# Last expert layer: groups of seven batches and one in place of six and two, denser scatters, one row tile less per group

## The chip, the cores and the metric

The kernel runs on one core of a Trainium2 chip. The metric is the device time of one execution in microseconds (us). The core has five engines that matter here: TensorE (PE, matmuls; PEld are its weight loads), VectorE (DVE), ScalarE (ACT), GpSimd (POOL) and SyncE (SP, which only issues DMAs). Each works through its own instructions in order. DMAs are issued from the queues of SP, ACT and POOL; the indirect ones (scatter and gather by row numbers) are issued from POOL.

## What is computed

The reference is a model of two layers over x of 8 batches x 512 tokens x 256 features. Layer 0 is sparse attention and a feed-forward layer of 32 experts with given choices. Layer 1 is a full attention, then another attention with 32 heads, then a mixture of 16 experts, which picks four per token by its own logits. Cut to the part that the change concerns:

```python
x = x + o @ wo                                   # the last attention, all 8 batches
h = _rms(x, ff_ln_w)
logits = h @ wg                                  # 16 experts
topv, topi = jax.lax.top_k(logits, TOP_K)        # four per token
gate = jax.nn.softmax(topv, -1)
a = silu(h @ w1[e]) * (h @ w3[e]);  y = a @ w2[e]   # for each chosen expert e
return x + sum over the four of gate * y
```

Every token goes to four experts, so 8 x 512 x 4 = 16384 rows of 256 numbers are computed, grouped by expert.

## The kernel before

Tokens are handled in tiles of 128, four to a batch (NT = 4). The kernel runs through its stages one after the other: layer 0's attention, `middle` (layer 1's first attention, with layer 0's experts between its steps), `attention2` (the last attention), and `experts1` (its experts).

**How rows get to experts.** `places` (L302) turns the choices of a group of tokens into row numbers, so that each expert's rows lie together and each expert starts on a new tile of 128 rows. It compares choices with expert numbers (L310), sums over tokens with a scan (L318), subtracts a triangle product (L328), does some twenty small operations on 16 columns, adds and masks on POOL (L355, L356) and reduces (L359). Its width is experts x tiles x choices: 16 x 24 x 4 = 1536 columns for six batches, 16 x 8 x 4 = 512 for two. `scatter` (L367) then writes 128 tokens for one of the four choices to their rows in DRAM, `row_tiles` (L380) runs the experts over tiles of 128 rows, and `gather` (L375) fetches the results back, 128 tokens and one choice at a time. One batch needs 4 x 4 = 16 scatters and 16 gathers.

**Pacing.** Each scatter and gather waits for the instruction that `ex["pace"]` held when it was written (L363): in `attention2` the latest exponential (L1225), in `row_tiles` the latest Silu (L404) or the latest copy of turned rows (L413).

**Groups.** The layer's experts run over two groups of batches (L44): batches 0 to 5, then 6 and 7. `R1` (L45) is the number of row tiles of each, and is fixed: tokens x choices / 128, plus 16 for the experts' started tiles, so 6 x 16 + 16 = 112 and 2 x 16 + 16 = 48. `R0` (L46) is the same for layer 0 with 32 experts: 96. All tiles are computed, filled or not.

**attention2.** For each batch there are eight steps (`sg`) of four heads. Their main work is written in a fixed order: scores (L1211), softmax (L1221 on VectorE, L1225 on ACT, L1232 on VectorE), transposes (L1262), values (L1282), output (L1290, L1291). Between its parts `serve` (L1315) lets other work go on. There are two lists. `side` holds what the next steps need: `queries`, `keys`, `kv_values`, `output`, and from step 4 on the `prologue` of the next batch. `slow` holds `after(b)` of finished batches: `gating` (L1383: norm, logits, the four choices, gates) and, after the last batch of group 0, `by_expert` (L1425), that is `places` in one go and then the scatters, one per step of the generator. Each call of `serve` makes one step of `side`, or of `slow` if `side` is empty, and every second call one more step of `slow`.

`rotated` (L1146) makes rotated queries and keys: two products on TensorE (L1154), four on VectorE (L1155, L1156), a difference and a sum on POOL (L1159, L1160), and eight small DMAs on SP (L1164). On POOL the scatters stand in the same queue as these.

**experts1** (L1445). First come `gating` of batch 7, the load of all expert weights (16 DMAs on SP, L1460), and `by_expert` of group 1. Then `row_tiles` runs over the tiles of group 0 and of group 1 in one sequence. A tile is loaded (L389), turned (L392, L394), multiplied with the weights of its expert (L402), passed through Silu and a product (L404, L405), turned (L411, L413), multiplied (L419) and stored (L421, L422); three tiles are in flight. The generator stops twice per tile. From the end of group 0's tiles on (L1504), each stop makes one step of `combine(0)` (L1469): one gather, and 15 gathers later its addition (L1476). At the first row of each batch, ACT issues the loads of `xr` and `acc` (L1487, L1488; two buffers each), and after a batch's last addition come two operations (L1479, L1480) and the output's store on SP (L1481). What is left of `combine(0)` after the last tile, and then all of `combine(1)`, follows behind the tiles. At the moment of the switch `combine(0)` is started twice, so there is one gather more than needed.

Of the kernel before, what the change touches and what calls it, by code (L numbers as in the profile page):

```python
# [21 lines left out]
B, S, D = 8, 512, 256  # L22
NT = S // P
# [11 lines left out]
E0, K0 = 32, 4  # L35
B0 = 4
# [4 lines left out]
SC2 = 1.0 / 8.0  # L41
E1, K1 = 16, 4

GROUPS = [range(0, B - 2), range(B - 2, B)]  # L44
R1 = [len(g) * NT * K1 + E1 for g in GROUPS]  # L45
R0 = B0 * NT * K0 + E0  # L46


def shape_constants():
# [110 lines left out]
def program(ctx: ExitStack, tc: tile.TileContext, a: dict, out: bass.AP):  # L160
# [53 lines left out]

    rows1 = [[dp.tile([n * P, D], F32, name=f"rows1_{w}{g}", tag=f"rows1_{w}{g}") for w in "xy"] for g, n in enumerate(R1)]
    rows0 = [dp.tile([R0 * P, D], F32, name=f"rows0_{w}", tag=f"rows0_{w}") for w in "xy"]

# [910 lines left out]
    def attention2():  # L1128

        with ExitStack() as cx:  # L1130
# [171 lines left out]
            def after(b):  # L1302

                yield from gating(b, wk, lambda: w2.tile([P, 2, S], F32, name="hf", tag="ts", bufs=1), (pT, "T"), (pmm, "mm"))
                for gi, g in enumerate(GROUPS):
                    if b == g[-1]:
                        yield from by_expert(gi, wk, pair, (pmm, "mm"))

            side, slow, count = [], [], [0]

            def step(todo):
                if todo and next(todo[0], StopIteration) is StopIteration:
                    todo.pop(0)

            def serve(n=1):  # L1315

                for _ in range(n):
                    count[0] += 1
                    step(side or slow)
                    if count[0] % 2:  # L1320
                        step(slow)

            last, oTs = None, []
# [18 lines left out]
                return PT  # L1342

            for b in range(B):
                for sg in range(8):
                    if sg < 7:
                        side.insert(0, queries(b, sg + 1))
                    if sg == 1:
                        side.append(kv_values(b, 1))
                    if sg == 2:  # L1350
                        side.insert(0, keys(b, 1))
                    if sg == 4 and b + 1 < B:
                        side.append(prologue(b + 1))
                    PT1 = second_half() if last else None
                    serve()
                    a0 = scores_a(b, sg, 0)
                    if last:
                        pair_values(0, last[2])
                    lb = scores_b(b, sg)
                    serve()  # L1360
                    PT0 = exponentials()
                    turn(PT0, *a0, lb, 0)
                    serve()
                    a1 = scores_a(b, sg, 1)
                    if last:
                        pair_values(1, PT1)
                        if last[1] % 2:
                            side.append(output(last[0], last[1], oTs))
                            oTs = []
                    serve(2)  # L1370
                    while sg < 7 and ("q", sg + 1) not in state[b] or sg == 7 and side:
                        step(side)
                    last = (b, sg, PT0, a1, lb)
# [9 lines left out]
    def gating(b, pool, hT, psT, psm):  # L1383
# [24 lines left out]
        for i in range(NT):  # L1408
            nc.vector.max(m8[:, i, :], lg[:, i, :])
            nc.vector.max_index(i8[:, i, :], m8[:, i, :], lg[:, i, :])  # L1410
        for gi, g in enumerate(GROUPS):
            if b in g:
# [12 lines left out]
    def by_expert(gi, pool, big, psm):  # L1425

        g, pu, ne = GROUPS[gi], ex["pu"][gi], E1
        nt = len(g) * NT
# [16 lines left out]
    def experts1():  # L1445


        with ExitStack() as cx:
# [12 lines left out]
            for _ in last:  # L1461
                pass
            ng = len(GROUPS[-1]) * NT * K1 * E1
            for _ in by_expert(len(GROUPS) - 1, cp, lambda n: cp.tile([P, ng], F32, name=n, tag=n), (po, "o")):
                pass
# [83 lines left out]
```

## Time and profile before

| | us |
|---|---|
| median of 3 runs (lowest, highest) | 5092.31 (5092.24, 5099.65) |
| the profiled execution | 5130.46 |
| its span, first to last instruction | 5128.8 |
| busy: PE, PEld, DVE, ACT, POOL | 4519.2, 2521.0, 2935.3, 2138.2, 1219.0 |
| mean granted clock of TensorE | 0.934 |
| end of batch 5, 6, 7 of `attention2` (last L1291) | 4034.4, 4291.7, 4499.0 |
| last matmul | 5070.7 |
| start of the first and of the last gather of `experts1` | 4910.8, 5118.8 |

The profile is of one execution. A line such as `L402 PE MATMUL g<-wall,xT` names the line of the kernel, the engine, the operation, and output and inputs by the program's names. A bracket such as `[2.89 <-DVE lf L1232]` says that the engine was idle for 2.89 us before it, and what ended that. The ends of matmuls are modelled, not seen. A granted clock of 1.00 is the full clock of TensorE, 0.5 the half. A line that begins with two times and a colon is a stretch of the span, with its length and each engine's busy time in it.

### The profile page before, as it was taken

What the parts mean: (1) busy time and instruction counts of PE and PEld (TensorE: products, weight loads), DVE (VectorE), ACT (ScalarE), POOL (GpSimd) and SP (SyncE); (2) the same over time, 40 slices, a digit from 0 to 9 for tenths busy, and PEclk for the clock granted to TensorE, in tenths of its full rate; (3) what the DMA queues carried; (4) which work ended last, traced back from release to release, by engine and by line L of the source; (5) the groups of instructions that cost most, each with busy time, mean ns of one, the idle gap of its engine ahead of it and who ended that gap; (6) DMA issues with size and microseconds to landing.
All of it is one profiled execution on the core that took longest, in us unless ns stands there. A gap on an engine that the chain in (4) does not pass through costs nothing.

```text
span 5128.8 us, 74283 instructions
## 1 busy us (share of the span) xinstructions
PE 4519.2 (88%) x25326; PEld 2521.0 (49%) x25326; DVE 2935.3 (57%) x8302; ACT 2138.2 (42%) x5688; POOL 1219.0 (24%) x1441
## 2 busy tenths in 40 slices
PE   5898999899999987897869999999999999959994
PEld 3444444444444443564435555555555555536652
DVE  3656565656566563434547666676767766622235
ACT  0243434343433433552216555555555545513331
POOL 3223232423131211004222111111201133220046
PEclk7898999999999988998989999999999999979997
DMA  2200000000011203333111011111101112152255
GB/s 60 92 16 26 8 27 7 28 8 27 8 56 42 88 3 116 110 99 87 35 70 32 25 32 26 28 26 27 36 22 29 29 49 63 47 206 88 87 159 174
DMA packets 199732, 281.76 MB, mean 55 GB/s; under 512 B 64912, under 2 KB 151312, under 8 KB 198464
## 3 DMA queue, kind: packets, MB, share of 16 engines
q1 hardware_dynamic: 175984, 208.70, 13.5%
q0 software_dynamic: 18480, 50.49, 3.1%
q10 hardware_dynamic: 4896, 17.83, 0.9%
q8 instruction: 207, 3.39, 0.3%
q14 instruction: 165, 1.35, 0.1%
HBM read 155.69 MB, written 109.15 MB: 52 GB/s over the span
## 4 chain that ended last, share of the span: by engine, by line
PE 61%; DVE 19%; ACT 6%; issue 5%; POOL 4%; DMA 3%; SPq 0%; another core or an unknown queue 0%; ACTq 0%; DVEq 0%; POOLq 0%
PE g L402 6%; PE pt L1262 5%; PE py L1290 5%; PE ps L1211 4%; DVE lf L1232 4%; PE ps L701 4%; PE pf L837 3%; PE po L1282 3%; PE o L419 3%; PE pq L1154 3%; ACT lf L1225 3%; PE po L810 2%; DVE lf L1221 2%; PE pf L842 2%; PE pt L636 1%
## 5 line engine op out<-in xcount | busy, mean ns | idle before, releaser
L858 ACT ACTIVATE e<-pf 128x512 f32<-128x512 f32 x896 | 464.3, 602 | 692.6 <-PE pf L848 287.6
L1225 ACT ACTIVATE lf<-lf,nm 128x512 f32<-128x512 f32 (+3 forms) x1024 | 566.7, 554 | 352.0 <-DVE nm L1221 342.6
L1221 DVE CUSTOM_DVE_ANT_0 lf<-ps,caus 128x512 f32<-128x512 f32 (+3 forms) x1024 | 449.7, 485 | 136.0 <-PE ps L1211 131.2
L709 DVE TENSOR_REDUCE bm<-ps 128x32 f32<-128x512 f32 (+1 forms) x704 | 403.3, 633 | 199.6 <-PE ps L707 198.9
L1262 PE MATMUL pt<-ident,lf 128*128 128x128 f32 x2560 | 379.7, 283 | 98.3 <-ACT PT L1268 48.2
L1211 PE MATMUL ps<-kT,qT 64*128 64x512 f32 (+3 forms) x2048 | 454.1, 466 | 0.1
L1232 DVE TENSOR_SCALAR lf<-lf,nm 128x512 f32<-128x512 f32 (+3 forms) x1024 | 434.1, 481 | 7.3
L1262 PEld LDWEIGHTS pt<-ident,lf 128*128 128x128 f32 x2560 | 290.7, 143 | 292.0 <-ACT PT L1268 133.6
L402 PE MATMUL g<-wall,xT 128*128 x1024 | 413.1, 526 | 11.7 <-DVE sg L405 5.6
L837 PE MATMUL pf<-XT,KT 32*128 32x512 f32 x1280 | 296.1, 685 | 75.2 <-DVE tm L780 66.9
L1160 POOL TENSOR_TENSOR tc<-tc,ts 128x512 f32<-128x512 f32 x80 | 103.4, 1292 | 1052.2 <-issue 633.5
L1282 PE MATMUL po<-PT,VT 128*64 128x384 f32 (+3 forms) x2048 | 330.5, 441 | 0.1
L701 PE MATMUL ps<-KT,qT 32*128 32x256 f32 (+3 forms) x2048 | 265.8, 504 | 60.9 <-ACT e L858 47.9
L376 POOL DMA_INDIRECT yk<-rows_y,pu x193 | 194.4, 1007 | 501.3 <-ACT y L421 343.3
L1211 PEld LDWEIGHTS ps<-kT,qT 64*128 64x128 f32 x2048 | 219.5, 187 | 155.3 <-issue 111.3
L405 DVE TENSOR_TENSOR sg<-sg,g 128x256 f32<-128x256 f32 (+1 forms) x256 | 94.9, 371 | 338.4 <-ACT sg L404 301.3
L1154 PE MATMUL pq<-hT,wq 128*128 128x512 f32 x512 | 260.0, 621 | 6.8 <-DVE ts L1156 5.9
L404 ACT ACTIVATE sg<-g 128x256 f32<-128x256 f32 (+1 forms) x256 | 88.2, 345 | 385.7 <-PE g L402 283.2
L1290 PE MATMUL py<-wo,oT 128*128 128x256 f32 x1024 | 240.3, 387 | 0.8 <-DVE x L1291 0.8
L1268 ACT COPY PT<-pt 128x512 f32<-128x512 f32 x256 | 148.6, 580 | 214.6 <-PE pt L1262 202.0
L1282 PEld LDWEIGHTS po<-PT,VT 128*64 128x64 f32 x2048 | 144.9, 136 | 187.7 <-issue 156.0
L402 PEld LDWEIGHTS g<-wall,xT 128*128 128x128 f32 x1024 | 177.7, 193 | 110.5 <-issue 80.2
(317 smaller groups left out, 7953.4 us busy)
## 6 DMA issues: line engine op xcount, KB each, us to landing
xt<-rows_x SPq DMA_DIRECT2D x256, 128.0 KB
rows_y<-y SPq DMA_DIRECT2D x256, 128.0 KB
qT<-tc SPq DMA_DIRECT2D x512, 64.0 KB
wall<-in_we SPq DMA_DIRECT2D x32, 768.0 KB
kT<-tc SPq DMA_DIRECT2D x128, 64.0 KB
xr<-spill ACTq DMA_DIRECT2D x9, 512.0 KB
acc<-spill ACTq DMA_DIRECT2D x9, 512.0 KB
xb<-in_x SPq DMA_DIRECT2D x8, 512.0 KB
```

The source lines that it names most:

```text
L402: nc.tensor.matmul(g, xT[:, k, :], wall[:, bass.ds(e, 1), k * 2 * I:(k + 1) * 2 * I], start=k == 0, stop=k == 1)
L701: nc.tensor.matmul(ps[hq][:, g * n:(g + 1) * n], qT[rows(hq), hh, g0 + g, :], kt[rows(hq), 0, hh, 64:64 + n], start=g == 0, stop=False, sk ...
L837: nc.tensor.matmul(ps[hq], kt[rows(hq), 0, hh, 64 + j * P:64 + (j + 1) * P], x[rows(hq), hh].rearrange("p g t -> p (g t)"), start=True, st ...
L858: ex["pace"] = nc.scalar.activation(e, ps[hq], AF.Exp, scale=SC0)
L1154: nc.tensor.matmul(pq, w[:, k, col + c * P:col + (c + 1) * P], hT[:, k, :], start=k == 0, stop=k == 1)
L1211: nc.tensor.matmul(ps[h][:, o:o + n], qT[rows, pr, i * P:(i + 1) * P], kT[rows, pr, :n], start=True, stop=True)
L1221: nc.vector.tensor_tensor_reduce(out=lf, in0=ps[h][:, o:o + n], in1=caus[:, S - n:], scale=-SC2, scalar=BIG, op0=ALU.add, op1=ALU.min, acc ...
L1225: ex["pace"] = nc.scalar.activation(lf, lf, AF.Exp, scale=-1.0, bias=nm[:, 0, u:u + 1], accum_out=nm[:, 1, u:u + 1])
L1232: nc.vector.tensor_scalar(lf, lf, nm[:, 1, u:u + 1], None, ALU.mult)
L1262: nc.tensor.transpose(pt[:, j * P:(j + 1) * P], x, ident)
L1282: nc.tensor.matmul(po[64 * h:64 * h + DH2, j * P:], v[:, j, 2 * pr + h, :], PT[h][:, j, j * P:], start=j == 0, stop=j == NT - 1, skip_grou ...
L1290: nc.tensor.matmul(py[:, u, :], oTs[c][:, (i + u) * P:(i + u + 1) * P], wo2[:, 2 * (sg - 1) + c, :], start=c == 0, stop=c == 3)
```

## The change

Group 0 has the batches 0 to 6, group 1 only batch 7. `places` for group 0 is then 16 x 28 x 4 = 1792 columns wide, for group 1 256. Both `R1` and `R0` lose one tile per group: 7 x 16 + 15 = 127 and 16 + 15 = 31, in sum 158 for 160, and 95 for 96. (16 experts share out a multiple of 128 rows, so at most 15 tiles more are started than filled.) `by_expert` of group 0 starts after batch 6, not 5; its scatters are 112 instead of 96, and all lie in batch 7. In batch 7 `serve` makes one more step of `slow` at each call: one at every call, and another at every second. Group 1 has 16 scatters and 16 gathers, for 32 and 32.

```diff
-GROUPS = [range(0, B - 2), range(B - 2, B)]
-R1 = [len(g) * NT * K1 + E1 for g in GROUPS]
-R0 = B0 * NT * K0 + E0
+GROUPS = [range(0, B - 1), range(B - 1, B)]
+R1 = [len(g) * NT * K1 + E1 - 1 for g in GROUPS]
+R0 = B0 * NT * K0 + E0 - 1
...
-            side, slow, count = [], [], [0]
+            side, slow, count, late = [], [], [0], [False]
...
                 for _ in range(n):
                     count[0] += 1
                     step(side or slow)
-                    if count[0] % 2:
+                    if late[0] or count[0] % 2:
+                        step(slow)
+                    if late[0] and count[0] % 2:
                         step(slow)
...
             for b in range(B):
+                late[0] = b == B - 1
                 for sg in range(8):
```

In the changed program's GpSimd order the instructions of batch 6 are those of an ordinary batch; in batch 7 the rotations follow runs of 14, 4, 7, 19, 17 and 19 scatters, and 28 scatters come after the last.

## The prediction

> **What bounds the kernel now.** I read the page first, then the windows by batch of the last attention, then the timeline inside one batch, then the end of the expert stage. The page's chain is mostly TensorE:
>
> ```profile
> PE 61%; DVE 19%; ACT 6%; issue 5%; POOL 4%; DMA 3%; SPq 0%; another core or an unknown queue 0%; ACTq 0%; DVEq 0%; POOLq 0%
> ...
> L376 POOL DMA_INDIRECT yk<-rows_y,pu x193 | 194.4, 1007 | 501.3 <-ACT y L421 343.3
> ```
>
> The change touches three stretches. First, batches 6 and 7 of the last attention. These windows end where x has its last product added (L1291): batch 5, an ordinary one, then 6, then 7. The columns are the length, the busy time and count of PE, weight loads, DVE, ACT and POOL, the granted clock, DMA share and GB/s.
>
> ```profile
> 3811.90:4034.40 222.50, 211.35 (x1106) 126.69 (x1105) 153.87 (x521) 128.64 (x407) 33.48 (x26) 1.00 0.11 27
> 4034.40:4291.70 257.30, 233.19 (x1114) 135.88 (x1113) 171.99 (x540) 131.32 (x407) 88.59 (x87) 0.94 0.17 51
> 4291.70:4499.00 207.30, 190.15 (x996) 113.53 (x994) 130.75 (x434) 115.70 (x362) 58.74 (x57) 0.97 0.16 47
> ```
>
> Batch 6 is 34.8 us longer than batch 5 with the same matmuls, and its clock is lower. It holds the ordering of group 0 (`places`) and 55 scatters; batch 7 has 41 scatters and no prologue of a next batch. Why a scatter costs anything is seen inside batch 6:
>
> ```profile
> 4145.78 0.96 POOL L369 DMA_INDIRECT rows_x<-x,pu  x1 [2.31 <-ACT lf L1225]
> ...
> 4146.58 3.61 DVE L1232 TENSOR_SCALAR lf<-lf,nm 128x384 f32<-128x384 f32 x4
> ...
> 4146.77 1.27 POOL L1160 TENSOR_TENSOR tc<-tc,ts 128x512 f32<-128x512 f32 x1
> 4147.99 1.26 POOL L1159 TENSOR_TENSOR tc<-tc,ts 128x512 f32<-128x512 f32 x1
> ...
> 4150.15 1.09 PE L1262 MATMUL pt<-ident,lf 128*128 128x128 f32 x4 [2.89 <-DVE lf L1232]
> ```
>
> The scatter waits for its pacing exponential, the rotation (L1160, L1159) stands behind it on GpSimd, and so it lands on the four normalisations, which take 3.61 us here and 1.14 us elsewhere; TensorE waits 2.89 us and then has the half clock for 6.8 us. In the attention's timeline a 128x384 normalisation takes 416 ns (median of 128) where GpSimd does nothing, 416 ns (27) beside a scatter, and 1418 ns (99) beside a tensor_tensor. So the scatters themselves take nothing from VectorE; the rotations they displace do.
>
> Second and third, the expert stage: steady row tiles, group 1's tiles with the gathers of group 0 among them, and the tail (same columns).
>
> ```profile
> 4578.00:4911.00 333.00, 333.00 (x1323) 205.35 (x1323) 93.52 (x221) 112.66 (x331) 0.20 (x1) 1.00 0.28 88
> 4911.00:5071.00 160.00, 143.68 (x543) 86.50 (x541) 76.73 (x176) 46.57 (x138) 91.28 (x94) 0.97 0.64 187
> 5071.00:5129.00 58.00, 0.00 (x0) 0.00 (x0) 32.40 (x56) 0.15 (x1) 38.04 (x36) 0.53 0.52 161
> ```
>
> TensorE is full in the first; a tile takes 3.02 us (start to start of L402). In the tail only gathers are left, and they set the end.
>
> **Part by part.** The sum is made against the profiled execution (span 5128.8, 5130.46 us with what lies around it), which is 38.2 us over the median of 5092.31; I carry the difference over unchanged.
>
> *One tile less, three times.* Layer 0's tiles at the end of their run follow each other in 1.82 us on a TensorE without gaps (2331.9 to 2333.7): -1.8. Layer 1 loses two, at 3.02: **-6.0**. Each takes one load and one store on SP with it (0.32 and 0.38 us of issue), which hide behind the tiles. The zero fills stay 12 and 20.
>
> *Batch 6* loses ordering and scatters. Its GpSimd order becomes batch 5's, so its length should: 222.5 for 257.3, **-34.8**.
>
> *Batch 7* takes the ordering of seven batches and 112 scatters. The ordering's DVE time, from batch 6's rows: L310 2.91, three scans 3.75, three L328 2.07, L359 2.73, together 11.5; some 17 small ones 2.9; and four L1232 that take 3.37 for 1.14 beside L355/L356, 2.2. That is 16.6, and with the wide ones times 7/6, 18.5. VectorE is the releaser of TensorE's waits there, so it lies on the path: **+18.5**. The scatters: of batch 6's 34.8, 18.2 are left for eight rotations displaced. Batch 7 already has displaced rotations; its clock of 0.97 (6 us) and about 6 us more of waits than batch 5 make some 10 us. After the change it has the same seven rotations after the ordering's start, behind runs of 4 to 19 scatters instead of 1 to 10. Bounds: all rotations slip clear of the normalisations, -10; cost in proportion to the scatters (10 x 112/41), +17. I take 0: the nearest row is batch 7 itself, the number of rotations is unchanged, and a scatter beside a normalisation costs it nothing. GpSimd then has 112 x 1.27 = 142 us of scatters, about 27 of rotations and others and 8 of the ordering, 177 of some 226: a rotation can stand up to ten scatters (13 us) late, while its qT is needed about 20 us on, after 5.6 us of DMA issue. That cover is thin; if it goes, it is the third rival.
>
> [...]
>
> *Front of the expert stage.* 32 scatters become 16 and end 16 x 1.27 = 20.3 us earlier. Until 4543 the expert weights load at about 400 GB/s, and that is unchanged. Behind it TensorE stands:
>
> ```profile
> 4557.25 1.88 PE L402 MATMUL g<-wall,xT 128*128 x4
> 4569.13 0.69 PE L411 MATMUL pt<-ident,sg 128*128 128x128 f32 x2 [10.00 <-issue]
> ```
>
> Six tiles take from 4545.9 to 4577.9 where 3.02 us each would give 4560.9: 17 us lost. ACT's L404 comes 15 us after its matmul was recorded, with no cause in the trace; the last scatter ends at 4567.5, 1.7 us before TensorE goes on. Bounds: 0 (the scatters only happen to be there) to -17. I take 0: 96 scatters and 129 gathers elsewhere hold no matmul so.
>
> *Group 1's tiles.* ACT issues the loads of xr and acc in its own order, and waits there until the output two batches earlier is written; Silu stands behind it, and TensorE behind that:
>
> ```profile
> ACT sg L404 <- DMA out<-acc: 25.6, 4, 7.5
> ```
>
> From L402's starts the four cost TensorE 5.65, 6.08, 6.10 and 1.54 us. In the changed ACT order only two such load pairs lie among the tiles (16 and 24 tiles into group 1); the others follow the last tile. **-7.6.**
>
> *The tail.* Two gathers go out per tile. 48 tiles carried all 96 of group 0; 31 carry 62 of 112. So 50 of group 0 and 16 of group 1 follow the last tile, where there were 32: 34 more. What a gather costs there:
>
> ```profile
> 5068.28 0.95 POOL L376 DMA_INDIRECT yk<-rows_y,pu  x1 [2.32 <-ACT sT L413]
> ...
> 5077.35 1.13 POOL L376 DMA_INDIRECT yk<-rows_y,pu  x1 [0.30 <-DVE acc L1476]
> ...
> 5118.76 0.95 POOL L376 DMA_INDIRECT yk<-rows_y,pu  x1 [0.30 <-issue]
> ```
>
> From 5077.35 to 5118.76 are 31 steps, 1.336 us each: 0.95 of work, 0.30 between, and delays by VectorE's adds. 34 x 1.336 = **+45.4** (bounds 42.5 at 1.25, 46.4 at the 1.364 from 5068.28 on). A batch of 16 then takes 21.4 us; loading acc and writing out take about 5 us each, so two buffers suffice. Nothing hides this: TensorE is done.
>
> Sum: -1.8 - 6.0 - 34.8 + 18.5 + 0 + 0 - 7.6 + 45.4 = +13.7 us. 5092.3 + 13.7 = **5106**; the profiled execution would be 5144.
>
> **Rivals.** *The front's stall goes* with the scatters: -17 more, -3 in all, 5089. For it: its end beside the last scatter's. Against: it is 10 us without any recorded wait, and may belong to that execution alone. *Batch 7 costs more*: rotations arrive late for the next scores: +17, 5123. For it: GpSimd at 177 of 226 us. Against: the 20 us between a rotation and its use. *Batch 7 absorbs the move*, and the change is faster: VectorE is busy 63% of batch 7 against 69% of batch 5, no prologue competes, so the ordering hides (-18.5) and the rotations come clear (-10): -14.8 in all, 5078. It decides from the point where batch 7 is no longer than 201.9 us (207.3 - 5.4, since the rest of the sum is -34.8 + 30.0 = -4.8). Against: the same ordering was not hidden in batch 6. *The scatters don't fit into batch 7* and run into the expert stage: the first row load waits for the last of them, 28 us after the batch ends; only beyond 22 left over would each cost 1.27 us. In the changed order 28 follow the last rotation, a whole step of heads before the end, so I give this nothing of its own.
>
> **Chances.** The forecast 0.50, the front's stall 0.20, batch 7 dearer 0.18, batch 7 absorbs 0.12. What a measurement can tell from no change is about 0.2%, 10 us. The forecast alone reaches from 5096 to 5117 (bounds of the tail and half of those of the rotations); about 0.13 of it is within 10 us. Faster 0.12, same 0.33, slower 0.55. The range takes in the front's case and the dearer batch: 5084 to 5126.
>
> **What would show it.** Batch 6 at 222 us with a clock of 1.00; batch 7 at about 226; two waits of ACT for the output instead of four; no matmul in the last 103 us instead of 58, with 66 gathers behind the last tile's at 1.34 us. Wrong if the gathers run ahead of the tiles, if batch 7 is under 202 or over 240 us, or if the steady tiles start much less than 79 us (4499 to 4578) after the attention's end.

## The result, and the profile after

The changed kernel takes 5120.57 us (median of 5 runs, 5118.95 to 5121.56), the kernel before in the same set 5092.31 (5088.69 to 5099.65): a ratio of 1.0054, with a 95% interval of 1.0042 to 1.0065. The change costs 28.3 us, 0.54%. The forecast was 5106, 13.7 us slower.

Three of the forecast's lengths can be read at once. First the windows of the last attention in the changed kernel, batch 5, 6 and 7, with the columns as in the prediction:

```profile
3806.03:4028.95 222.92, 212.81 (x1106) 127.89 (x1105) 153.81 (x520) 128.70 (x407) 33.44 (x26) 0.99 0.11 27
4028.95:4251.44 222.49, 211.34 (x1106) 126.72 (x1105) 152.21 (x516) 128.58 (x407) 28.76 (x24) 1.00 0.11 27
4251.44:4478.45 227.01, 200.91 (x1006) 117.75 (x1004) 142.31 (x459) 115.18 (x362) 135.74 (x136) 0.95 0.26 84
```

Batch 6 is an ordinary batch at full clock (222.5), batch 7 takes 227.0 where about 226 was forecast, and all of group 0's work on GpSimd (136 instructions for 57 before) lies in it. Then the windows of the expert stage: from the attention's end to the first row tile, the tiles of group 0, group 1's tiles with the gathers, and the tail.

```profile
4478.45:4524.40 45.95, 6.79 (x28) 5.06 (x28) 10.30 (x51) 2.57 (x4) 18.69 (x26) 0.53 0.99 399
4524.40:4910.00 385.60, 385.03 (x1521) 236.76 (x1522) 108.00 (x256) 128.30 (x378) 0.20 (x1) 0.99 0.29 91
4910.00:5014.01 104.01, 97.25 (x377) 59.35 (x376) 47.57 (x110) 32.45 (x96) 56.33 (x59) 0.98 0.61 175
5014.01:5117.20 103.19, 0.00 (x1) 0.00 (x0) 53.79 (x95) 0.37 (x1) 72.97 (x71) 0.52 0.55 168
```

TensorE is full from the first tile on (385.03 of 385.60): the 10 us stall at the front is not there. The last 103.19 us hold no matmul, where 103 were forecast. On the page, GpSimd's share of the chain and the costliest group of gathers stand beside those shown of before:

```profile
PE 62%; DVE 19%; ACT 6%; issue 5%; POOL 5%; DMA 4%; SPq 0%; ACTq 0%; DVEq 0%; POOLq 0%
...
L376 POOL DMA_INDIRECT yk<-rows_y,pu x193 | 194.5, 1008 | 528.3 <-ACT sT L413 421.7
```

The gathers are as many and as long as before (1008 ns for 1007); what grew is the idle time ahead of them, behind the tiles (421.7 us put down to L413). They start late, not slow.

And yet the two traces do not show the result. The span of the changed kernel's profile is 5117.2 us, that of before 5128.8: by the traces the change gains 11.6 us, by the medians it costs 28.3. The profiled execution of before was 38.2 us over its median, and the prediction carried that difference over "unchanged". Where it lies was the first question.

### The profile page after: what moved, and what is told of

Its sections match the earlier page's. It is cut to its first block, busy times and chain, and to the rows that moved or that the text cites. A ratio compares the mean times of both kernels' runs of the same rounds, so it can differ in the third digit from the quotient of the medians.

```text
span 5117.2 us, 74167 instructions
## 1 busy us (share of the span) xinstructions
PE 4504.5 (88%) x25295; PEld 2514.8 (49%) x25295; DVE 2924.8 (57%) x8298; ACT 2131.3 (42%) x5679; POOL 1218.9 (24%) x1441
## 4 chain that ended last, share of the span: by engine, by line
PE 62%; DVE 19%; ACT 6%; issue 5%; POOL 5%; DMA 4%; SPq 0%; ACTq 0%; DVEq 0%; POOLq 0%
PE g L402 7%; PE pt L1262 5%; PE py L1290 5%; PE ps L701 4%; PE ps L1211 4%; PE po L1282 3%; DVE lf L1232 3%; PE pf L837 3%; PE pq L1154 3%; PE o L419 3%; ACT lf L1225 3%; PE po L810 3%; DVE lf L1221 2%; PE pf L842 2%; PE ph L582 1%
## 5 line engine op out<-in xcount | busy, mean ns | idle before, releaser
L1211 PE MATMUL ps<-kT,qT 64*128 64x128 f32 (+3 forms) x2048 | 448.5, 461 | 0.1
L402 PE MATMUL g<-wall,xT 128*128 x1012 | 404.8, 523 | 12.5 <-DVE sg L405 6.1
L1282 PE MATMUL po<-PT,VT 128*64 128x384 f32 (+3 forms) x2048 | 330.3, 440 | 0.1
L376 POOL DMA_INDIRECT yk<-rows_y,pu x193 | 194.5, 1008 | 528.3 <-ACT sT L413 421.7
L1154 PE MATMUL pq<-hT,wq 128*128 128x512 f32 x512 | 261.1, 624 | 18.0 <-DVE ts L1156 17.1
L404 ACT ACTIVATE sg<-g 128x256 f32<-128x256 f32 (+1 forms) x253 | 86.8, 343 | 368.3 <-PE g L402 339.1
L1290 PE MATMUL py<-wo,oT 128*128 128x256 f32 x1024 | 238.8, 386 | 0.8 <-DVE x L1291 0.8
L1282 PEld LDWEIGHTS po<-PT,VT 128*64 128x64 f32 x2048 | 145.3, 136 | 187.5 <-issue 155.0
L402 PEld LDWEIGHTS g<-wall,xT 128*128 128x128 f32 x1012 | 174.5, 192 | 108.3 <-issue 77.1
```

The costliest lines, as they stand in the source:

```text
L402: nc.tensor.matmul(g, xT[:, k, :], wall[:, bass.ds(e, 1), k * 2 * I:(k + 1) * 2 * I], start=k == 0, stop=k == 1)
L1154: nc.tensor.matmul(pq, w[:, k, col + c * P:col + (c + 1) * P], hT[:, k, :], start=k == 0, stop=k == 1)
L1211: nc.tensor.matmul(ps[h][:, o:o + n], qT[rows, pr, i * P:(i + 1) * P], kT[rows, pr, :n], start=True, stop=True)
L1282: nc.tensor.matmul(po[64 * h:64 * h + DH2, j * P:], v[:, j, 2 * pr + h, :], PT[h][:, j, j * P:], start=j == 0, stop=j == NT - 1, skip_grou ...
L1290: nc.tensor.matmul(py[:, u, :], oTs[c][:, (i + u) * P:(i + u + 1) * P], wo2[:, 2 * (sg - 1) + c, :], start=c == 0, stop=c == 3)
```

## The experiments

The runs of one set share one chip, and each set has its own runs of the kernel before. That turned out to matter: in two sets, and beside the result, the kernel before has medians of 5092.3 to 5092.7 us; in the other two 5131.75 and 5143.74, like the first profile's 5130.46. Below they are called chips of the first and of the second kind; whether it is the chip, or something else that lasts through a set, is not shown (the records of the four sets name four different chips, 6 and 0 for the first kind, 14 and 10 for the second, and none twice). Times are compared within a kind only.

### The kernel before once more (first kind)

No edit.

> The kernel before, unchanged, once more with a profile of its own. Its profiled execution took 38.2 us more than its median, the changed kernel's took no more than its median; so the two traces show -11.6 us where the medians show +28.3. Theory A: the 38 us belong to that one execution. Then this profile has a span near 5092, and some of the stretches of before are shorter in it: above all the expert stage up to the last matmul, which was 571.7 us in the profile of before (535.6 in that of the changed kernel, 36 less, where 13.6 were forecast). The 10.0 us stall at the front of the expert stage (17 us from six tiles) would be gone, with 32 scatters still there. Theory B: the stall at the front belongs to the 32 scatters, and is in every execution of this kernel: then it stands here too, between the first tiles, and the 38 us are elsewhere.

Median 5095.53, ratio 1.0001 (0.9992 to 1.0010), span of the profile 5092.9. The windows of batch 5, 6 and 7 in it:

```profile
3805.34:4027.84 222.50, 211.36 (x1106) 126.72 (x1105) 153.85 (x520) 128.66 (x407) 33.46 (x26) 1.00 0.11 27
4027.84:4275.61 247.77, 227.91 (x1114) 131.53 (x1113) 174.53 (x541) 130.07 (x407) 88.52 (x87) 0.97 0.18 53
4275.61:4477.56 201.95, 187.16 (x996) 111.33 (x994) 131.31 (x434) 115.29 (x362) 58.61 (x57) 0.98 0.16 48
```

and its expert stage, in the same four parts:

```profile
4477.56:4522.60 45.04, 7.22 (x28) 5.06 (x28) 12.03 (x51) 2.57 (x4) 17.15 (x24) 0.53 0.99 400
4522.60:4875.00 352.40, 351.94 (x1389) 216.63 (x1390) 98.81 (x235) 117.31 (x345) 20.16 (x22) 0.99 0.31 98
4875.00:5035.26 160.26, 145.99 (x532) 88.22 (x530) 76.16 (x174) 45.42 (x135) 88.39 (x91) 0.91 0.65 183
5035.26:5092.90 57.64, 0.00 (x0) 0.00 (x0) 32.73 (x57) 0.37 (x1) 37.73 (x36) 0.54 0.53 164
```

The stall at the front is gone (351.94 of 352.40), with all 32 scatters still there. Against the first profile, 7.1 us are missing ahead of batch 1, 9.6 in batch 6 (257.3 to 247.8), 5.3 in batch 7 (207.3 to 202.0) and 14.0 from the attention's end to the last matmul (571.7 to 557.7): together 36.0. Theory A's lengths hold, theory B's do not. But the reason theory A gave, that one execution had lost the time, falls below.

This profile is the right partner for the changed kernel's. Together they give +24.3 us: batch 6 -25.3, batch 7 +25.1, from the attention's end to the last matmul -22.1, the tail +45.6, and +1.1 in all that lies ahead.

### One row tile less, alone (first kind)

```diff
-R1 = [len(g) * NT * K1 + E1 for g in GROUPS]
-R0 = B0 * NT * K0 + E0
+R1 = [len(g) * NT * K1 + E1 - 1 for g in GROUPS]
+R0 = B0 * NT * K0 + E0 - 1
```

> The kernel before with one row tile less per group alone (R1 of 111 and 47 instead of 112 and 48, R0 of 95 instead of 96). Theory of the prediction: -1.8 and two times -3.02, so -7.8 us against the kernel before, about 5084. Rival: the tiles at the end of group 1 hide the gathers, so that one tile less there only moves two gathers into the tail at 1.34 us each: then -1.8 -6.0 +2.7 = -5.1, about 5087. Together with the rest of the change (+36 us by the medians, if it is +28.3 with this) it says how much grouping and density cost by themselves.

5082.7, ratio 0.9984 (0.9973 to 0.9995), -9.8 us against 5092.48. That is the -7.8 of the forecast within the interval (-13.8 to -2.5); the rival's -5.1 is inside too, so the two are not told apart. In the traces the rival's two gathers are there, 38 behind the last matmul for 36, but the tail is only 1.5 us longer (59.2 for 57.6), and from the first tile's L402 to the last matmul it is 9.8 us shorter (500.9 for 510.7). Grouping and density by themselves then cost about 28.3 + 9.8 = 38 us.

### All scatters of group 0 behind batch 7 (first kind)

```diff
-                        yield from by_expert(gi, wk, pair, (pmm, "mm"))
+                        work = by_expert(gi, wk, pair, (pmm, "mm"))
+                        yield next(work)
+                        while not ended[0]:
+                            yield
+                        yield from work
...
+            ended[0] = True
             while slow:
```

> The changed kernel with all 112 scatters of group 0 behind batch 7: the ordering (places) stays where it is, the scatters begin when the last step of heads has been written. It tells the ordering's price in batch 7 from that of the scatters. Theory of the prediction: the ordering lies on the path with 18.5 us, and the scatters cost batch 7 as much as before (some 10 us over no scatters): batch 7, 227.0 us long in the changed kernel, becomes 227 - 10 = 217. Rival: the ordering is mostly hidden and the runs of scatters ahead of the rotations cost most of the 20 us (one rotation behind 18 scatters holds VectorE 11.5 us at L1156 and TensorE 10.9): batch 7 becomes 205 or less. In both, the first row load then waits for 112 scatters at 1.27 us, 142 us, of which some 15 lie before the attention's end, where the expert weights take 45 us anyway: the whole becomes some 70 to 85 us longer, 5190 to 5205.

5192.91, ratio 1.0196 (1.0183 to 1.0210), inside the range given. Batch 7 of this kernel, in which 13 of the scatters still lie, behind the last rotation:

```profile
4240.96:4457.41 216.45, 199.45 (x1006) 117.30 (x1004) 140.89 (x460) 115.13 (x362) 40.39 (x37) 0.97 0.10 28
```

216.4 us, where the prediction's theory said 217 and the rival 205 or less. With dense62 below, whose batch 7 has neither ordering nor scatters of group 0 and takes 196.6, this prices both: the ordering 216.4 - 196.6 = 19.8 us, on the path as forecast (18.5), and the scatters ahead of the rotations 227.0 - 216.4 = 10.6. Nearly all of the 10.6 is one wait, by the trace; no run of the first kind took this wait away alone. The timeline of the changed kernel's batch 7, on GpSimd, VectorE and TensorE:

```profile
4318.11 0.69 DVE L1155 TENSOR_TENSOR tc<-pq,cos 128x512 f32<-128x512 f32 x1 [0.24 <-PE pq L1154]
...
4326.81 0.96 POOL L369 DMA_INDIRECT rows_x<-x,pu  x1 [0.30 <-issue]
4327.80 1.27 POOL L1160 TENSOR_TENSOR tc<-tc,ts 128x512 f32<-128x512 f32 x1
4329.02 1.26 POOL L1159 TENSOR_TENSOR tc<-tc,ts 128x512 f32<-128x512 f32 x1
...
4330.31 0.69 DVE L1156 TENSOR_TENSOR ts<-pq,sin 128x512 f32<-128x512 f32 x1 [11.51 <-POOL tc L1159]
...
4331.06 3.78 PE L1154 MATMUL pq<-hT,wq 128*128 128x512 f32 x4 [10.92 <-DVE ts L1156]
```

The first rotation stands behind 18 scatters. The next rotation's sine product (L1156) writes the same `ts`, which has one buffer, and cannot start until L1159 has read it. VectorE stops for 11.5 us, and TensorE, whose next product (L1154) waits for L1156, which reads `pq`, for 10.9.

### Four gathers per tile instead of two (first kind)

```diff
                     next(rest, None)
+                    next(rest, None)
```

> The changed kernel with four gathers per tile of group 1 instead of two (the generator of gathers is stepped twice at each stop). Theory of the prediction (the gathers set the tail, and TensorE has nothing left to do beside them): 31 tiles of 3.02 us, 94 us, can carry 94/1.27 = 74 gathers instead of 62, and the 12 more leave the tail at 1.336 us each: -16 us, about 5104; if ACT's waits for the output (L1487, L1488) then also hold the tiles back to the pace of the gathers, 112 gathers take 142 us beside the tiles and the tail is 16 of them, 21 us and 5 for the output: 4915 + 142 + 26 = 5083. Rival: GpSimd is not what sets the tail (the additions on VectorE or the loads of the rows do), or the waits on ACT cost what is gained: no gain, 5117 to 5125. This is also a candidate for beating the changed kernel, and below 5092 for beating both.

5100.18, ratio 1.0015 (1.0006 to 1.0024): 20.4 us below the changed kernel, between the theory's two figures, and still 7.7 over the kernel before. The windows of group 1's tiles and of the tail:

```profile
4915.00:5058.56 143.56, 104.56 (x358) 60.78 (x356) 80.21 (x168) 31.90 (x92) 106.28 (x105) 0.92 0.67 203
5058.56:5099.70 41.14, 0.00 (x0) 0.00 (x0) 18.83 (x33) 0.37 (x1) 24.45 (x26) 0.54 0.46 147
```

The tail is 62 us shorter (41.14 for 103.19), but the last matmul comes 44.5 us later: TensorE is busy for 104.56 of 143.56 us there, and which of the waits beside the gathers holds it was not taken apart. So the gathers do set the end; dealing them faster returns 17.5 us by the spans and 20.4 by the medians, since 128 of them need, as an estimate, 160 us of GpSimd at 1.25 (0.95 of work and 0.30 between, the last gather of before) and the 31 tiles of group 1 last 94, at 3.02 each. The rival (another engine sets the tail) falls.

### Two buffers for `ts`; the ordering a batch later; the loads on SP's queue; all together (second kind)

```diff
-                ts_ = w2.tile([P, 2, S], F32, name="ts", tag="ts", bufs=1)
+                ts_ = w2.tile([P, 2, S], F32, name="ts", tag="ts", bufs=2)
```

(`hf` of the norm, which has the same tag, gets two buffers with it.)

> The changed kernel with two buffers for ts (the sine product of the rotations) instead of one. In batch 7 of the changed kernel a rotation stands behind 18 scatters on GpSimd, and VectorE waits 11.5 us at L1156 for it, because the next sine product goes into the same buffer; TensorE waits 10.9. With all scatters behind the batch, batch 7 took 216.4 instead of 227.0. Theory: the scatters' whole price in batch 7 is this one wait, so batch 7 becomes 216 to 217 and the whole 10.5 us shorter, about 5110. Rival: the late rotation holds the next scores up anyway (its qT is used some 20 us on), so the wait only moves: batch 7 stays at 224 to 227, the whole at 5118 to 5121.

In wait62, against the changed kernel, the groups are those of before, and the ordering starts after batch 6:

```diff
-GROUPS = [range(0, B - 1), range(B - 1, B)]
+GROUPS = [range(0, B - 2), range(B - 2, B)]
...
-                    if b == g[-1]:
+                    if b == g[-1] + 1:
```

> Groups of six and two as before, but group 0 is ordered and scattered a batch later (after batch 6 instead of 5), with the changed kernel's density in batch 7 and its one tile less per group. It separates the move of the ordering into batch 7 from the sizes of the groups: the tail of 32 gathers and the four waits of ACT stay as before. In the second profile of the kernel before batch 6 is 247.8 and batch 7 202.0 us, together 449.7; in the changed kernel 222.5 and 227.0, together 449.5. Theory: the move by itself gains nothing, so against the kernel before only the tiles count (measured -9.8), and 16 scatters and 256 columns of places fewer in batch 7 than in the changed kernel bring 2 to 4 us more: 5079 to 5083. Rival (the prediction's sum from the first profile): the move gains 34.8 - 18.5 = 16 us: 5066 to 5070.

sp62 is the kernel with one tile less per group, with

```diff
-                    nc.scalar.dma_start(xr, spill[b])
-                    nc.scalar.dma_start(acc, spill2[b])
+                    nc.sync.dma_start(xr, spill[b])
+                    nc.sync.dma_start(acc, spill2[b])
```

> The kernel before with one tile less per group (5082.7) and with the loads of xr and acc issued from SP's queue instead of ACT's. Theory: the four waits of ACT for an output written two batches earlier, with Silu behind them, cost TensorE 6.05, 7.04, 6.29 and 6.40 us in the second profile of the kernel before, 25.8 together, and on SP nothing that TensorE needs within 6 us stands behind them (the rows are loaded up to six tiles ahead): 5082.7 - 25.8 = 5057, if the tail stays at 57.6. Rival: the gathers of group 0 then fall behind the shorter run of tiles (47 tiles in 142 us for 96 gathers at 1.27, 122 us), or SP's waits hold up the loads of rows and the stores of y, and TensorE loses the same there: 5075 to 5083.

> All together: groups of six and two, the ordering of group 0 after batch 6 with the changed kernel's density, one tile less per group, two buffers for ts, and the loads of xr and acc on SP's queue. If the terms add: 5082.7 for the tiles, -25.8 for ACT's four waits, -10.5 for the wait at ts in batch 7, 0 to -3 for the move by itself: 5043 to 5047, 45 us below the kernel before. If the waits only move (SP for ACT, scores for ts): 5075 to 5083.

The kernel before took 5131.75 in this set, and against it:

| kernel | median, us | ratio (interval) | batch 6 | batch 7 |
|---|---|---|---|---|
| ts2 | 5193.87 | 1.0131 (1.0113, 1.0149) | 222.6 | 295.8 |
| wait62 | 5173.07 | 1.0083 (1.0068, 1.0098) | 222.5 | 286.1 |
| sp62 | 5104.34 | 0.9944 (0.9931, 0.9957) | 257.1 | 207.2 |
| best | 5146.79 | 1.0034 (1.0023, 1.0044) | 222.6 | 285.4 |

The three kernels with dense scatters missed all their numbers, by 64 us and more. The kernel before is 39 us slower in this set too, but that is not it: their batch 7 takes 285 to 296 us, where 216 to 227 were expected. So nothing can be said from this set on the theories given for them. sp62, with the scatters as before, has batches 6 and 7 of the first profile to 0.3 us:

```profile
4025.09:4282.15 257.06, 232.90 (x1114) 135.87 (x1113) 171.81 (x541) 131.41 (x407) 88.66 (x87) 0.94 0.17 51
4282.15:4489.34 207.19, 190.20 (x996) 113.47 (x994) 130.76 (x434) 115.68 (x362) 58.74 (x57) 0.97 0.16 47
```

So the first profile's extra time was no accident of one execution: it is how the kernel runs in such a set. That is where theory A's reason falls. Of the versions that were run, sp62 and the kernel with one tile less alone beat the kernel before beside them, sp62 by 27.4 us (the changed kernel was not in its set). ACT shows no wait for the output any more, TensorE stands for 1.0 us in all between 4905 and its end, and the sum fits what its own kind of chip had to lose: in the first profile the four waits cost 5.65, 6.08, 6.10 and 1.54 us, 19.4, and with 7.8 for the tiles that is 27.2 (the 35 us expected were made from the second profile). By the traces the fit is looser, and the move of the loads does one thing more. The issue of the 16 loads of expert weights on SP, in the first profile and in that of sp62:

```profile
4498.99 26.76 SPq L1460 DMA_DIRECT2D wall<-in_we  x16
```

```profile
4489.37 19.73 SPq L1460 DMA_DIRECT2D wall<-in_we  x16
```

In the first profile 17.3 us of waits for the loads of `xr` and `acc`, which ACT issues at the attention's end, lie among them; in sp62 these loads stand behind the weights, and the first row tile starts 35.8 us behind the attention for 45.0 (36.3 in best, which has the same loads, and 45.0 in wait62, which has not). At the sixth tile, behind this kind's stall, 3.8 us of that are left. From there to the last matmul sp62 is 26.3 us shorter (6.0 for two tiles, so 20.3 for the waits), and its tail is 2.1 longer. It was not measured on a chip of the first kind, where no stall hides the earlier start.

### The changed kernel and ts2 once more (second kind)

No further edit.

> The changed kernel, unchanged, beside the kernel before on the chip of this set. The kernel before took 5092.5 us in one set of runs and 5131.75 in the next, and its two profiles differ in the same way: batch 6 is 247.8 us in one and 257.3 in the other, batch 7 202.0 and 207.2, and the 10 us stall at the front of the experts is in one only. The set where it is slow had the two kernels with dense scatters in batch 7 (two buffers for ts; the ordering one batch later), and there batch 7 took 295.8 and 286.1 us. Theory: this is the chip and the runs of scatters, not those edits: ACT stops about 6 us after an unbroken run of scatters has begun and TensorE goes on within 3 us of its end. Then, where the kernel before takes about 5130, the changed kernel's batch 7 takes 285 to 296 us and the whole 5180 to 5195, over 1% slower than before; where it takes about 5092, the first result repeats (227 us and 5119 to 5122). Rival: the edits themselves made batch 7 long: then the changed kernel has 227 us in batch 7 here too, and is 20 to 30 us slower than the kernel before on either chip.

> The changed kernel with two buffers for ts, once more, beside the changed kernel on the same chip. On a chip where the kernel before takes about 5092: batch 7 becomes 216 to 217 for 227.0 and the whole 10 us shorter than the changed kernel, if the scatters' whole price there is the one wait at L1156; no shorter, if the rotation holds up the next scores anyway. On a chip where it takes about 5130, theory (the runs of scatters stop the engines, whatever the buffers): within 5 us of the changed kernel there. Rival (the second buffer itself, which lets VectorE run ahead, makes batch 7 long): 60 us or more above the changed kernel.

The kernel before 5143.74; the changed kernel 5216.44, ratio 1.0142 (1.0122 to 1.0162); with two buffers for `ts` 5216.75, ratio 1.0133 (1.0113 to 1.0153). Here the change costs 72.7 us, and a second `ts` changes nothing. Both theories held for the side and, but for 0.6 us, for batch 7; the whole is 21 us over the 5180 to 5195 given, where the kernel before is 12 slower than in the set that these were made from. Both rivals (the edits made batch 7 long) fell. Batch 7 of the changed kernel, to be read against 227.01 above:

```profile
4261.27:4557.86 296.59, 213.66 (x1006) 125.01 (x1004) 137.12 (x459) 116.46 (x362) 136.04 (x136) 0.85 0.20 64
```

The same instructions, with about as much work on VectorE, ACT and GpSimd, in 69.6 us more. TensorE stands 56.8 us longer, and its work takes 12.8 us more at a mean clock of 0.85. One of the stops, on GpSimd, TensorE and ACT, in the middle of the eight products of L1290:

```profile
4407.97 0.99 POOL L369 DMA_INDIRECT rows_x<-x,pu  x1 [0.17 <-issue]
...
4411.45 2.37 PE L1282 MATMUL po<-PT,VT 128*64 128x512 f32 x16
...
4413.76 1.56 PE L1290 MATMUL py<-wo,oT 128*128 128x256 f32 x6
...
4414.56 0.96 POOL L369 DMA_INDIRECT rows_x<-x,pu  x1 [0.30 <-issue]
...
4424.69 0.96 POOL L369 DMA_INDIRECT rows_x<-x,pu  x1 [0.31 <-issue]
4425.38 0.59 ACT L1334 COPY oT<-po 128x512 f32<-128x512 f32 x1 [11.14 <-remote]
4425.96 0.96 POOL L369 DMA_INDIRECT rows_x<-x,pu  x1 [0.30 <-issue]
4426.01 2.50 PE L1290 MATMUL py<-wo,oT 128*128 128x256 f32 x5 [10.70 <-issue]
```

TensorE stops for 10.70 us between two products of one sum. The view names no cause for it ("issue", "remote"), but the instructions carry the semaphores (counters that one engine raises and another waits for) that they wait for: TensorE's next weight load one that ACT raises, and it starts 0.05 us after L1334's end; L1334 one that only TensorE raises, which reaches it at 4425.35, 11.5 us after the recorded end of the last product that it copies (L1282, 4413.82). GpSimd scatters all the while, 15 in a row from 4408.0 to 4426.9. It is much the same in the long runs of this batch from 4370 on. ACT stops 5.5 to 6.2 us after the beginning of the four runs of 15 and 17 scatters, and TensorE goes on, the run of 10 behind them included, at 4391.0, 4426.0, 4468.9, 4506.1 and 4539.0, where the runs end at 4391.5, 4426.9, 4470.0, 4505.5 and 4535.3; the stops are 13.0, 10.7, 12.5, 12.2 and 6.6 us.

In the run before these, 18 scatters from 4315.2 to 4337.9, TensorE stands for 11.2 us, hardly more than the 10.9 at `ts` on the first kind. The stall of the first profile, from 4559.1 to 4569.1 beside scatters that ended at 4567.5, looks like one more: ACT's L404 starts 14.9 us after its product's recorded end (4553.37 to 4568.24), with ACT idle for 12.2 of them. All four profiles of the second kind with 32 scatters there (the first one, sp62, wait62, best) have such a stall among the first six tiles, the three with 16 have none, and none of the first kind has one. On the chip of the first kind a run of 19, from 4410.3 to 4434.3, holds nobody up, with TensorE busy for 22.3 of the 24.0 us; ACT's line of the changed kernel there:

```profile
4415.49 0.56 ACT L1334 COPY oT<-po 128x512 f32<-128x512 f32 x1
```

In the kernel before no run in the attention is longer than 7, which fits its smaller loss on the second kind.

What stops the engines is not settled. What can be read is where the wait begins: in the four stops at runs of 15 and 17, L1334 starts 9.7 to 13.0 us after the recorded end of its product, with ACT idle for 9.3 to 12.6 of them; in batch 7 on the first kind it never starts later than 0.4 us after both its product and ACT's instruction before it. Either TensorE's signal comes late or its products end later than the record, whose ends are modelled, has them.

A second guess was instructions that come late. They come by DMA as well: the page of the changed kernel lists a queue of kind "instruction" with 207 transfers, of 16 KB each in the trace (a second one, with 165, was not followed). In the changed kernel's batch 7 on the first kind they fall inside runs of scatters (4369.8 in the run from 4359.6 to 4383.6, 4391.8 in 4386.3 to 4407.6, 4418.2 in 4410.3 to 4434.3); on the second, of the five from 4370 on four come after a run's end (4395.5, 4432.0, 4507.3, 4540.0; the fifth, 4456.6, inside one). That would fit an engine that has run out of instructions, and it is an argument only: TensorE goes on up to 6 us before such a transfer is recorded, ACT and TensorE each start within 0.1 us of the signal that they wait for, and no run changed the instruction loads.

### The density alone, and the groups alone (first kind)

dense62 has groups of six and two, with the density from batch 6 on; sparse is the changed kernel without density. Both have one tile less per group.

```diff
-GROUPS = [range(0, B - 1), range(B - 1, B)]
+GROUPS = [range(0, B - 2), range(B - 2, B)]
...
-                late[0] = b == B - 1
+                late[0] = b >= B - 2
```

> Groups of six and two with the ordering after batch 5, as in the kernel before, but with the changed kernel's density from batch 6 on, and one tile less per group: the density alone. GpSimd's order then has the 96 scatters in runs of 18, 1, 10, 19, 11, 1, 15 and 21 ahead of rotations, nearly all in batch 6, none in batch 7. Theory (the unbroken runs of scatters cost, not the groups): where the kernel before takes about 5130 to 5145, TensorE stops 10 to 13 us in each run of 15 or more and a few us in those of 10, so batch 6 grows from 257 to 300 to 320 us, batch 7 falls from 207 to about 197, and the whole is 25 to 50 us over the kernel before; where it takes about 5092, batch 6 grows by one wait of some 11 us at the buffer of ts, batch 7 falls to about 197, and the whole is within 6 us of the kernel with one tile less (5083). Rival (what batch 7 pays in the changed kernel comes from the groups: 112 scatters of seven batches, the wider ordering): density costs batch 6 nothing, and the whole is 8 to 18 us below the kernel before on either chip.

```diff
-                late[0] = b == B - 1
+                late[0] = False
```

> The changed kernel without the density: groups of seven and one alone. The runs ahead of rotations in batch 7 are then 4, 3, 1, 10, 8 and 10 scatters, and 76 follow the last rotation, in the last step of heads and behind it. Where the kernel before takes about 5092: batch 7 217 to 222 us, and the first row tile waits for 76 scatters (97 us, of which some 20 beside the last step and 45 beside the weights' load): 5130 to 5145. Where it takes about 5130 to 5145, theory (runs beyond some five scatters stop the engines until their end): the runs of 8 and 10 cost 4 to 6 us each, some 16, and the last run of 76 stands across the attention's last step, so that it ends 50 to 80 us late, but the row tiles then wait no longer for scatters: 5190 to 5230, no better than the changed kernel. Rival (density alone is to blame): batch 7 at 222 to 230 there, and the whole at 5165 to 5180.

The kernel before took 5092.70 here. dense62: 5094.24, ratio 1.0000 (0.9991 to 1.0009), 11.5 us over the same groups without density (5082.7), where at most 6 were expected. Its batches 6 and 7:

```profile
4025.61:4285.90 260.29, 227.35 (x1114) 133.65 (x1113) 164.04 (x541) 129.52 (x407) 128.06 (x128) 0.94 0.23 71
4285.90:4482.50 196.60, 185.75 (x996) 113.33 (x994) 124.23 (x433) 114.60 (x362) 19.67 (x16) 0.98 0.09 22
```

260.3 + 196.6 = 456.9, for 244.7 + 202.0 = 446.7 in the kernel with one tile less. In its batch 6 the waits of TensorE's L1154 for L1156 alone sum to

```profile
PE pq L1154 <- DVE ts L1156: 19.8, 3, 14.5
```

the longest 14.5 us: again the rotation behind a run of scatters. The rival (density costs a batch nothing) falls.

sparse: 5146.84, ratio 1.0106 (1.0091 to 1.0122), 26.3 us over the changed kernel. Batch 7 takes 221.3 us, in the range given; the whole is 2 us above its range. The wait for the scatters comes by another way than I had said, ahead of the row tiles already: the rms norm of batch 7's `gating` has two small operations on GpSimd (L266, L267), and these stand behind the 50 scatters that are left when the attention ends:

```profile
PE pT L1401 <- DVE x L1395: 65.1, 1, 65.1
DVE x L1395 <- POOL rms_r L267: 62.0, 1, 62.0
```

So of the four combinations, all with one tile less, two groups of six and two take 5082.7 (thin) and 5094.2 (dense), seven and one 5146.8 (thin) and 5120.6 (dense). The density costs 11.5 us with the one and saves 26 with the other; the better of seven and one is 38 us over the better of six and two.

## Why the prediction was right, and where it was not

The side was right and the change gains and costs in the places named; the size was half of the measured one (13.7 for 28.3). 5120.6 lies above the 5096 to 5117 that the forecast's own case allowed, and inside the stated 5084 to 5126, which took in the dearer batch. Term by term, against the second profile of before, which has the conditions of the medians:

| step of the sum | forecast | measured | by |
|---|---|---|---|
| layer 0's tile | -1.8 | not to be told | the stretch up to the end of batch 0 is 2905 to 2917 us in seven profiles of the first kind |
| batch 6 | -34.8 | -25.3 | 247.8 to 222.5 |
| batch 7: ordering | +18.5 | +19.8 | send less dense62 |
| batch 7: rotations | 0 | +5.2 | 227.0 - 216.4 = 10.6 in the changed kernel, 202.0 - 196.6 = 5.4 for 41 scatters before |
| front | 0 | +0.9 | 45.0 to 46.0 |
| two tiles of layer 1 and two waits of ACT | -13.6 | -23.0 | first tile to last matmul, 512.7 to 489.6 |
| tail | +45.4 | +45.6 | 57.6 to 103.2 |

Measured, the lines from batch 6 on sum to +23.2, and with +1.1 ahead to the 24.3 of the two traces; the medians say 28.3, and the 4 us between lie within what single executions of the kernel before spread (5080 to 5102). That the sum came within 8 us of this is partly luck: batch 6 brought 9.5 us less than forecast and the tiles with ACT's waits 9.4 more, so that the two errors cancel.

**The tail** is the step that decided, and it is right: 70 gathers start after the last matmul for 36, 34 more, at 1.335 us each (1.336 forecast).

**Batch 6** is the term that was mis-sized most, by 9.5 us. Its mechanism holds (222.5 us, full clock), but 257.3 was the length of a chip of the second kind, and the result came from one of the first kind, where batch 6 had been 247.8. The assumption that failed is the sentence that the 38.2 us are carried over "unchanged": 9.6 of them lay in the very stretch that the change removes, and could not be won by it. I had the two numbers that warned of it, 5130.46 and a highest run of 5099.65, and took no range from them.

**The rotations.** "The number of rotations is unchanged, and a scatter beside a normalisation costs it nothing" holds (in the changed kernel a 128x384 normalisation takes 410 ns beside a scatter, median of 21, and 416 with GpSimd idle, median of 134), and 0 was too little by 5.2. I gave a late rotation 20 us of cover, until its qT is needed; the buffer of `ts` is needed again after about 3 (2.8 in the changed kernel's batch 7, from the end of the rotation's L1156 at 4316.04 to that of the next L1155 at 4318.81). The cover was counted at the wrong reader: the next writer comes first.

**The two waits of ACT** were taken at 7.6 us from a profile in which the fourth cost 1.5. In the second profile the four cost 6.05, 7.04, 6.29 and 6.40. The waits themselves, in the profile of the kernel before run again and in that of the changed kernel:

```profile
ACT sg L404 <- DMA out<-acc: 27.3, 4, 7.6
```

```profile
ACT sg L404 <- DMA out<-acc: 12.9, 2, 6.7
```

Four became two, as said. Two of them are about 13 of the 17 us (23.0 - 6.0); TensorE's clock in that stretch, 0.91 before and 0.98 after, goes the way of the rest. It is about what single profiles of this stretch differ by: the two kernels of six and two with one tile less per group, tiles and dense62, have it 9.8 and 6.6 us shorter than the kernel before, where two tiles are 6.0.

**The rivals.** *The front's stall goes* was given 0.20, at 17 us. Its mechanism is real on the second kind: there the changed kernel has no stall between its first tiles (390.80 of 391.40 us busy), and the kernel before has one. On the first kind it has nothing to remove, so it gave nothing to the result. One of the prediction's own signs of being wrong hangs on it: the steady tiles start (the sixth tile) 62.8 us after the attention's end, much less than 79. The change did not do this, since the kernel before on the first kind has 61.8. *Batch 7 dearer* was named with the right place, the rotations behind GpSimd's scatters, and a total, 5123, that is near the measured one by luck: its 17 us came out as 5.2 on the first kind. On the second kind batch 7 is far dearer, 296.6 us for 207.3, and the change costs 72.7 us in all, outside the range I gave, but by another mechanism than late rotations: the stops above, which a second `ts` leaves as they are. *Batch 7 absorbs the move* is refuted by the ordering's 19.8 us; batch 7 would have had to stay under 201.9. That 112 scatters don't fit was right to leave aside: the first row tile started 46.0 us behind the attention for 45.0.

The 1.27 us that the prediction counted for a scatter held too: the 112 scatters in batch 7 keep 1.27 us from start to start (median), and the 45 of them that a normalisation overlaps take 0.986 us on average, the other 67 0.960.

## What to carry to other kernels

Before a sum is made from one profile, set its own time beside the runs: an excess sits somewhere, and if it sits in the stretch that the change removes, it cannot be won. When work is packed more densely into a queue, ask of each instruction behind it not only who reads its result but who next writes its inputs' buffers; here a single buffer made of a rotation behind 18 scatters a stop of three engines, VectorE for 11.5 us, TensorE for 10.9 and ACT for 13.3 (whether a second buffer gives the time back was not measured where the result was). And work whose last part lies with one engine alone, as the gathers lie with GpSimd here, should be dealt so that this engine is never idle ahead of it: seven and one moved 34 gathers behind the last tile, and the gains further up, 25 us in batch 6 and 23 in the tiles, did not pay for these 45 us and the 25 of batch 7.

## What the runs showed of the hardware that was not expected

- The kernel before took 5092 us in some sets and 5132 to 5144 in others, at a mean clock of 0.934 and 0.935 in its two profiles, and batches 1 to 5 at 222.5 us in both. What differs is the time beside scatters (in the two profiles 9.6 us in batch 6, 5.3 in batch 7, and the stall of 10.0 at the front of the experts); the stretch up to the end of batch 0 is 2912 to 2941 us in the seven profiles of the second kind and 2905 to 2917 in the seven of the first.
- In the sets of the second kind ACT, VectorE and TensorE stopped until about the end of five of the six unbroken runs of ten or more scatters in one batch, for 6.6 to 13.0 us on TensorE, although the scatters themselves take 1.27 us from start to start in both kinds; none from runs of up to 28 in the same batch on the first kind, but for the one at `ts`. In four of them ACT stood 9.3 to 12.6 us at a wait for TensorE's semaphore, after the recorded end of the product. The cause is open.
- Issuing the loads of `xr` and `acc` from SP instead of ACT removed the waits of Silu for an output that was still being written (25.6 us in four on ACT in the first profile, none in that of sp62), without a new one on SP that TensorE felt (SP waits 4.7 us in two for the output, TensorE stands for 1.0 in all there), and the first row tile started 9 us earlier, with 17.3 us of waits for them gone from the loads of the expert weights.
